# Fewer picked sets, more gathered chunks, and gathers placed behind evictions in a graph kernel

## The chip, the core and the metric

The kernel runs on one core of a Trainium2 chip. The engines that matter here are TensorE (PE in the profile; its weight loads are shown apart as PEld), VectorE (DVE), ScalarE (ACT), GpSimd (POOL) and SyncE (SP). Each works through its own list of instructions in order and waits on semaphores for the others. Time is device microseconds of one execution; the number given for a kernel is the median of its runs.

## The reference

One layer of message passing on a graph of 12,500 nodes with 128 features and 400,000 edges, followed by a residual sum and a layer norm. The edges come sorted by their destination `dst`; sources and types are random.

```python
Xs = X[src]
m_data = Xs @ W_data.T + b_data
m_ctrl = Xs @ W_control.T + b_control
msg = jnp.where((edge_types == 0)[:, None], m_data, m_ctrl)
agg = jax.ops.segment_sum(msg, dst, num_segments=X.shape[0])
out = agg + (X @ W_self.T + b_self)
x = _layernorm(x + jax.nn.relu(out), axis=-1)
```

## The kernel before

The sum over edges and the weights commute, so the kernel first adds up rows of `x` for every destination node and edge type, and applies the weights once per node. `x` is split into three bf16 parts that add up to the float32 value: `x3` on chip, `rows3` in DRAM (768 bytes a node).

**Chunks, windows, groups.** The edges are cut into 3125 chunks of 128, and these into NG = 25 groups of 125. A group consists of NE = 5 stretches of 5 + 20 chunks: a small window of PB = 5 chunks ("p") and a large one of EC = 20 chunks ("e"). The rows of x come to a chunk in one of two ways.

*Gathered* chunks: POOL issues one indirect DMA for each chunk (`fetch`, line 721), which brings the 128 source rows of its edges from `rows3` to a tile `msg`. PE adds them up by destination with three matmuls (line 677) against a 0/1 matrix `psel` made by DVE, and counts them with a fourth (line 753).

*Picked* sets: a whole e window of 20 chunks is handled as a set. DVE and PE rank its 2560 edges by the block of 128 nodes that their source lies in (the lines from 529 to 656) and put them into 25 slots (NQ) of 128 places; PE then picks rows of `x3` by matmuls with 0/1 matrices into PSUM tiles `got` (line 782), two slots to a pair, and ACT copies each pair to an SBUF tile `emsg` (line 793, the *eviction*; 12 in a set). PE adds them by destination (line 677) and counts (line 804). The few edges that fit no slot are gathered by one further indirect DMA of a set into the tile `last` (`spare_rows`, line 758), which is a part of the last slot.

In odd groups the fifth e window is no set: there the last p window has PL = 25 chunks, all gathered. So there are 13 x 5 + 12 x 4 = 113 sets and 13 x 25 + 12 x 45 = 865 gathered chunks.

**Buffers.** `got` has two PSUM buffers, each of one pair; `emsg` five; `msg` has HOLD = 18 tiles. `acc`, the sums of a group, has two buffers.

**Order.** The program is written out as one stream, and each engine gets its part of it in that order. The outer loop (line 991) runs over the sets w. A set has six turns (`unit`, line 813): in each, two pairs of slots are picked and evicted, and the four slots of the turn before are counted and added; the rest of a set is ended in the first turn of the next. Into this stream `merged` puts, by a fraction of the set: the gathered chunks, spread evenly over all sets from the third on (LAG = 2, line 983), the ranking for sets w+2 and w+3, the preparation of the next group's indices (`prep_p`, `prep_e`), and what a finished group still needs: `pass_on` and `finish`, which apply the weights and the norm and store four tiles of 125 nodes.

A chunk (`chunk`, line 741) lists at its place the gather of the chunk that comes AHEAD = 14 later; 14 gathers are listed ahead of the loop (line 974). Since `msg` has 18 tiles, such a gather writes to the tile of the chunk four places back, and waits until PE has read it. The spare gather of a set is listed in the set's third turn (line 825). POOL has hardly any work besides the gathers.

A chunk may only be gathered when its group's indices `codes["p", g]` are there, and a group is passed on to the next (`pass_on`, line 701) when all of its windows have been accumulated: 5 p windows and its sets.

Of the kernel before, what the change touches and what calls it, by code (L numbers as in the profile page):

```python
# [9 lines left out]
BF = mybir.dt.bfloat16  # L10
# [7 lines left out]
P = 128  # L18
D = 128
# [4 lines left out]
NG = NC // GC  # L24
GN = P * GC * N // E
PB = 5
PL = 25
EC = 20
CQ = EC // 4
NE = 5  # L30
NWIN = 2 * NE
# [12 lines left out]
NCELL = 4 * NQ  # L44
OVF = 64
TOP = 7
SB = 1
HOLD = 18
AHEAD = 14
ACC_ROWS = 99 * P  # L50
# [97 lines left out]
def evenly(units, a=0.0, b=1.0):  # L148
    return [(a + (b - a) * (k + 0.5) / len(units), u) for k, u in enumerate(units)]


def short_path(ctx, tc, const, ident, eps, wT, brow, bad, x, src, dst, etype, ws, bs, out):
    nc = tc.nc
# [11 lines left out]
    def windows(g):  # L165

        c = g * GC
        for i in range(NE):
            yield "p", i, c, PB
            yield "e", i, c + PB, EC  # L170
            c += PB + EC

    def of_p(g, i):

        return PL if g % 2 and i == NE - 1 else PB

    def edges(a, c, n):
        return a[c * P:(c + n) * P].rearrange("(p c) -> p c", c=n)

    rows_p = (NE - 1) * PB + PL  # L180
    each_e = [(g, i) for g in range(NG) for i in range(NE - g % 2)]
    raw = {}
    starts = {k: [c for kind, _, c, _ in windows(0) if kind == k] for k in "pe"}
    gap = PB + EC
# [37 lines left out]
    for kind, i, c, _ in windows(0):  # L222
        if kind == "p":
            n = PL if i == NE - 1 else PB
            nc.sync.dma_start(
                out=near_i[i * PB:i * PB + n, :],
                in_=dst.rearrange("(o g e) -> o g e", o=1, g=NG)[:, :, c * P].to_broadcast([n, NG]),
# [6 lines left out]
    rows3 = dram.tile([N, 3 * D], BF, name="rows3")  # L234
# [181 lines left out]
    codes = {}  # L416
# [61 lines left out]
    def select(sel, col, code2):  # L478

        rows, n, width = sel.shape  # L480
        shape = [rows, n, width // 2, 2]
        nc.vector.tensor_tensor(  # L482
            sel.rearrange("p n (w t) -> p n w t", t=2),
            col[:rows].rearrange("p (o w t) -> p o w t", o=1, t=2).to_broadcast(shape),
            code2.rearrange("p n (o t) -> p n o t", o=1).to_broadcast(shape),
            op=OP.is_equal,
        )
        return sel
# [178 lines left out]
    acc, added, parts_in = {}, [], {}  # L667

    def sums():
        return ps2.tile([P, 512], FP, name="sums")  # L670

    def cells_of(ps, width, k):
        return ps[:, k * 2 * width:(k + 1) * 2 * width]

    def add_rows(out, msg, sel, start, stop):
        for j in range(3):
            nc.tensor.matmul(  # L677
                out, msg[:, j * D:(j + 1) * D], sel, start=(start and j == 0), stop=stop, skip_group_check=True
            )
# [20 lines left out]

    def pass_on(g):

        assert parts_in[g] == NWIN - g % 2
        if g + 1 < NG:
            begin_acc(g + 1)
            added.append(nc.vector.tensor_add(acc[g + 1][:, :, :lap], acc[g + 1][:, :, :lap], acc[g][:, :, GN:]))
# [8 lines left out]
        added.append(nc.vector.tensor_add(win, win, ps[:, :4 * wide].rearrange("p (a w) -> p a w", w=wide)[:, :, :width]))  # L715


    to_fetch = [(g, i, c) for g in range(NG) for i in range(NE) for c in range(0, of_p(g, i), SB)]
    fetched = []

    def fetch():
        if to_fetch:
            g, i, c = to_fetch.pop(0)
            msg = mp.tile([P, SB, 3 * D], BF, name="msg")
            for k in range(min(SB, of_p(g, i) - c)):
                at = i * PB + c + k
                nc.gpsimd.indirect_dma_start(  # L727
                    out=msg[:, k, :], out_offset=None, in_=rows3[:, :],
                    in_offset=bass.IndirectOffsetOnAxis(ap=codes["p", g][0][:, at:at + 1], axis=0),
                )  # L730
            fetched.append(msg)

    def gathered(g, i):
        n = of_p(g, i)
        s = {}

        def choose():
            sel = sp.tile([P, PL, 2 * PW], BF, name="psel")[:, :n]
            s["sel"] = select(sel, near_col, codes["p", g][1][:, i * PB:i * PB + n])

        def chunk(c):
            if c % SB == 0:
                fetch()
                s["msg"] = fetched.pop(0)
            if c == 0:
                s["ps"] = sums()
                choose()
            sel = s["sel"][:, c].rearrange("p (t w) -> p t w", t=2)
            rows, cnt = (
                cells_of(s["ps"], AW, k).rearrange("p (t w) -> p t w", t=2)[:, :, DPC * c:DPC * c + PW] for k in range(2)  # L750
            )
            add_rows(rows, s["msg"][:, c % SB, :], sel, c == 0, c == n - 1)
            nc.tensor.matmul(cnt, one_col, sel, start=False, stop=(c == n - 1), skip_group_check=True)  # L753
            if c == n - 1:
                accumulate(g, 2 * i, s["ps"], AW, PW + DPC * (n - 1))

        return evenly([lambda c=c: chunk(c) for c in range(n)])

    def spare_rows(w):
        msg = slots[w]["last"] = two.tile([P, 3 * D], BF, name="last")  # L760
        nc.gpsimd.indirect_dma_start(  # L761
            out=msg[:OVF, :], out_offset=None, in_=rows3[:, :],
            in_offset=bass.IndirectOffsetOnAxis(ap=slots[w]["idx"], axis=0),
        )

    def picked(w, tiled, ending, fin_used, before):

        g, i = each_e[w]  # L770
        s = {"sel": {}, "msg": {}}
        per, pair = 4, 2

        def choose(q0, n=8):

            sel = select(sp.tile([P, 9, 2 * EW], BF, name="esel")[:, :n], code_col, slots[w]["code"][:, q0:q0 + n])
            for k in range(n):
                s["sel"][q0 + k] = sel[:, k]

        def pick(ps, q, a0=0):  # L780
            for a in range(a0, 4):
                nc.tensor.matmul(  # L782
                    ps[CAP * a:CAP * (a + 1), :], slots[w]["pick"][:, a * NQ + q, :],
                    x3[:, 4 * q + a - a0].rearrange("p j d -> p (j d)"), start=True, stop=True, skip_group_check=True,
                )

        def rows(q):
            ps = psg.tile([P, pair, 512], FP, name="got")
            msg = two.tile([P, pair, 3 * D], BF, name="emsg", bufs=5)
            for k in range(pair):  # L790
                pick(ps[:, k, :3 * D], q + k)
                s["msg"][q + k] = msg[:, k, :]
            nc.scalar.copy(msg, ps[:, :, :3 * D])  # L793

        def last_rows():
            q = NQ - 1
            ps = psg.tile([P, pair, 512], FP, name="got")[:, 0] if fin_used else ps1.tile([P, 512], FP, name="fin")
            pick(ps[:, :3 * D], q, 2)
            nc.scalar.copy(s["msg"][q][OVF:, :], ps[OVF:, :3 * D])

        def count(q):
            if q == 0:
                s["ps"] = sums()
            nc.tensor.matmul(  # L804
                cells_of(s["ps"], EW, 1)[CAP * (q % 4):CAP * (q % 4 + 1), :], one_col[:, :CAP], s["sel"][q],
                start=(q < 4), stop=(q + 4 >= NQ), skip_group_check=True,
            )

        def add(q0, q1):
            for q in range(q0, q1):  # L810
                add_rows(cells_of(s["ps"], EW, 0), s["msg"].pop(q), s["sel"][q], False, q == NQ - 1)

        def unit(t):

            for q in range(t * per, (t + 1) * per, pair):
                rows(q)
            if t == 1 and before:
                before()
            if t in (0, 1):
                choose(8 * t)  # L820
            if t == 0:
                ending()
            if t == 2:
                if w > 0:
                    spare_rows(w)
                s["msg"][NQ - 1] = slots[w]["last"]
            if t == 3:
                choose(16, 9)
            if t > 0:
                for q in range((t - 1) * per, t * per if t < turns - 1 else NQ):  # L830
                    count(q)
            if t == turns - 1:
                last_rows()
            if t > 0:
                add((t - 1) * per, t * per)
            for u in tiled.get(t, []):
                u()

        def end():

            add((turns - 1) * per, NQ)
            for u in tiled.get(turns, []):
                u()
            accumulate(g, 2 * i + 1, s["ps"], EW, EW)

        turns = (NQ - 1) // per
        return evenly([lambda t=t: unit(t) for t in range(turns)]), end


# [111 lines left out]
    mp = ctx.enter_context(tc.tile_pool(name="msg", bufs=HOLD))  # L961
# [9 lines left out]
    load(1, "p")  # L971
    for u in prep_p(0):
        u()
    for _ in range(AHEAD):
        fetch()


    chunks, closed, rest = {}, {}, []
# [1 line left out]
    n = 0  # L980
    for p in range(NG * NE):
        for _, u in gathered(*divmod(p, NE)):
            at = LAG + (n + 0.5) * (pairs - LAG) / total
            chunks.setdefault(int(at), []).append((at % 1, u))
            n += 1
        closed.setdefault(int(at), []).append(p)

    def ending():
        pass

    for w in range(pairs):
        g, i = each_e[w]
# [197 lines left out]
```

## Time and profile before

| | |
|---|---|
| time before, median of 3 runs (lowest, highest) | 2089.18 us (2087.51, 2096.8) |
| time of the profiled execution | 2084.42 us |
| its span, first to last instruction | 2082.7 us |
| mean granted clock of PE over the span | 0.986 |
| DMA traffic | 254.92 MB, mean 122 GB/s |
| sets / gathered chunks | 113 / 865 |

The page gives the busy time of each engine and its share of the span, then groups of instructions: line, engine, operation, what is written and read, the shapes and the count; behind the bar the busy time, the mean duration of one in ns, and the idle time of the engine just before them with what ended it. A wait is put down to the instruction whose semaphore came last. Matmuls are pipelined, so the busy time of PE covers more than the time in which its array is full, and the ends of matmuls are modelled. Line 677 is a helper of two callers; the tiles tell them apart: `esel,emsg` of picked sets, `psel,msg` of gathered chunks. Where lines of the profile are shown in windows, the columns are the length of the window, then busy us and instructions (x) of PE, PEld, DVE, ACT and POOL, the granted clock, the busy share of the DMA engines and GB/s.

### The profile page before, as it was taken

The numbers are of one execution on the slowest core, as the hardware profiler recorded it, in microseconds if no ns is written. First come the engines' busy times: TensorE is split into PE (matmuls) and PEld (weight loads), VectorE is DVE, ScalarE is ACT, GpSimd is POOL, SyncE is SP. The second block draws the span as 40 slices with busy tenths as digits, with TensorE's granted clock in tenths as the row PEclk, the third lists the DMA queues.
The fourth block names the chain that finished last, engine by engine and source line by source line (L and its number), as shares of the span: only waits on it lengthen the run. The fifth ranks groups of instructions, "written<-read, shape, count | busy, mean of one in ns | idle before, by whom it ended". The sixth has DMA issues, their size and how long they took to land.

```text
span 2082.7 us, 75459 instructions
## 1 busy us (share of the span) xinstructions
PE 1828.3 (88%) x30869; PEld 1369.9 (66%) x30869; DVE 1718.1 (82%) x4707; ACT 1304.3 (63%) x2464; POOL 1296.7 (62%) x996
## 2 busy tenths in 40 slices
PE   0489889999999998899998999999999999999996
PEld 0367666676666776676666666766776676776675
DVE  7689788988887888888888888878888888888873
ACT  3466666666665666666566666656666666766665
POOL 0446567667667667567666566676676676665660
PEclk9999999999999999999999999999999999999998
DMA  7534343443443443433433434434434434434331
GB/s 213 185 107 134 107 136 102 139 136 98 135 136 97 135 131 102 133 121 112 126 105 118 130 101 134 133 101 134 133 97 132 136 99 132 134 107 132 122 98 33
DMA packets 186535, 254.92 MB, mean 122 GB/s; under 512 B 85369, under 2 KB 152995, under 8 KB 183108
## 3 DMA queue, kind: packets, MB, share of 16 engines
q1 hardware_dynamic: 128418, 152.97, 22.7%
q0 software_dynamic: 45136, 90.65, 15.5%
q10 hardware_dynamic: 12626, 6.40, 1.1%
q8 instruction: 243, 3.98, 0.8%
q14 instruction: 112, 0.92, 0.1%
HBM read 231.89 MB, written 18.04 MB: 120 GB/s over the span
## 4 chain that ended last, share of the span: by engine, by line
PE 56%; DVE 30%; ACT 5%; issue 4%; DMA 2%; another core or an unknown queue 1%; DVEq 1%; SPq 0%; ACTq 0%
PE sums L677 24%; PE got L782 18%; ACT emsg L793 4%; DVE esel L482 4%; PE rk L620 3%; DVE pick L662 3%; DVE prod L570 3%; DVE rv L608 3%; PE sums L804 2%; DVE found L579 2%; DVE prod L548 2%; DVE ahead L566 2%; PE rk L556 2%; PE rk L508 1%; DVE half L575 1%
## 5 line engine op out<-in xcount | busy, mean ns | idle before, releaser
L727 POOL DMA_INDIRECT msg<-rows,pidx x865 | 1153.9, 1334 | 619.9 <-PE sums L677 251.9
L793 ACT CAST emsg<-got 128x768 bf16<-128x768 f32 x1356 | 1035.6, 802 | 494.2 <-PE got L782 371.4
L677 PE MATMUL sums<-esel,emsg 128*128 128x176 bf16 x8136 | 755.5, 241 | 11.4 <-issue 10.8
L782 PE MATMUL got<-x,pick 128*32 128x384 bf16 x10896 | 664.7, 332 | 91.8 <-ACT emsg L793 60.8
L677 PEld LDWEIGHTS <-emsg 128*128 128x128 bf16 x8136 | 598.1, 98 | 169.0 <-issue 152.5
L782 PEld LDWEIGHTS <-pick 128*32 128x32 bf16 x11074 | 260.8, 95 | 255.3 <-issue 156.0
L482 DVE TENSOR_TENSOR esel<-code_col,code 128x1408 bf16<-128x1408 bf16 x339 | 308.9, 911 | 29.0 <-PE sums L677 13.6
L715 DVE TENSOR_TENSOR acc<-acc,sums 128x352 f32 (+2 forms) x238 | 102.0, 429 | 169.2 <-PE sums L677 79.7
L761 POOL DMA_INDIRECT last<-rows,idx x113 | 138.7, 1227 | 132.8 <-DMA bias<-b_parts 71.3
L677 PE MATMUL sums<-psel,msg 128*128 128x48 bf16 x2595 | 186.0, 184 | 12.2 <-DVE acc L715 7.8
L804 PE MATMUL sums<-esel,one_col 128*32 128x176 bf16 x2825 | 183.5, 242 | 9.0 <-issue 8.4
L677 PEld LDWEIGHTS <-msg 128*128 128x128 bf16 x2595 | 149.1, 97 | 21.0 <-issue 18.1
L620 PE MATMUL rk<-rv,O 128*128 128x64 bf16 x2260 | 90.5, 195 | 68.0 <-DVE rv L608 63.8
L662 DVE TENSOR_SCALAR pick<-pick,lane_f 128x1600 bf16<-128x1600 bf16 x226 | 142.8, 637 | 6.8 <-DMA pick<-there 4.2
L482 DVE TENSOR_TENSOR O<-cell_col,blk 128x2000 bf16<-128x2000 bf16 x113 | 134.7, 1192 | 15.1 <-PE fin L782 6.3
L753 PE MATMUL sums<-psel,one_col 128*128 128x48 bf16 x865 | 145.3, 183 | 0.2 <-issue 0.2
L620 PEld LDWEIGHTS <-O 128*128 128x128 bf16 x2260 | 83.2, 100 | 93.9 <-issue 92.9
L570 DVE TENSOR_TENSOR prod<-O,ahead 128x2000 bf16<-128x2000 bf16 x113 | 134.4, 1190 | 0.0
L804 PEld LDWEIGHTS <-one_col 128*32 128x32 bf16 x2825 | 86.6, 96 | 45.8 <-issue 16.7
L566 DVE TENSOR_REDUCE ahead<-rk 128x100 bf16<-128x500 f32 x113 | 76.2, 675 | 48.6 <-PE rk L498 21.3
L753 PEld LDWEIGHTS <-one_col 128*128 128x128 bf16 x865 | 82.7, 96 | 1.2 <-issue 1.1
L579 DVE TENSOR_REDUCE found<-half 128x20 f32<-128x520 bf16 x113 | 77.4, 685 | 0.0
(173 smaller groups left out, 2026.6 us busy)
## 6 DMA issues: line engine op xcount, KB each, us to landing
pick<-there SPq DMA_DIRECT2D x113, 800.0 KB
acc<-acc_start SPq DMA_DIRECT2D x23, 1280.0 KB
msg<-rows,pidx POOLq DMA_INDIRECT x865
rows<-x SPq DMA_DIRECT2D x6, 1344.0 KB
xs<-in_x_dram SPq DMA_DIRECT2D x99, 62.5 KB
out_dram<-h SPq DMA_DIRECT2D x99, 62.5 KB
xt<-in_x_dram ACTq DMA_DIRECT2D x6, 896.0 KB
there<-cell SPq DMA_DIRECT2D x113, 6.2 KB
```

Source lines behind the costliest of these rows:

```text
L482: nc.vector.tensor_tensor(sel.rearrange("p n (w t) -> p n w t", t=2), col[:rows].rearrange("p (o w t) -> p o w t", o=1, t=2).to_broadcast( ...
L570: nc.vector.tensor_tensor(prod, s["O"], ahead.rearrange("p (o j) -> p o j", o=1).to_broadcast([P, EC, NCELL]), op=OP.mult)
L579: nc.vector.tensor_reduce(found, half[:, :, :26], AX.X, OP.add)
L620: nc.tensor.matmul(s["rk"][:m, :2 * CAP], s["held"][:, c * NCELL:c * NCELL + m], s["rv"][:, c].rearrange("p v r -> p (v r)"), start=(c == ...
L662: nc.vector.tensor_scalar(t, t, lane_f, None, op0=OP.is_equal)
L677: nc.tensor.matmul(out, msg[:, j * D:(j + 1) * D], sel, start=(start and j == 0), stop=stop, skip_group_check=True)
L727: nc.gpsimd.indirect_dma_start(out=msg[:, k, :], out_offset=None, in_=rows3[:, :], in_offset=bass.IndirectOffsetOnAxis(ap=codes["p", g][0] ...
L753: nc.tensor.matmul(cnt, one_col, sel, start=False, stop=(c == n - 1), skip_group_check=True)
L761: nc.gpsimd.indirect_dma_start(out=msg[:OVF, :], out_offset=None, in_=rows3[:, :], in_offset=bass.IndirectOffsetOnAxis(ap=slots[w]["idx"], ...
L782: nc.tensor.matmul(ps[CAP * a:CAP * (a + 1), :], slots[w]["pick"][:, a * NQ + q, :], x3[:, 4 * q + a - a0].rearrange("p j d -> p (j d)"), ...
L793: nc.scalar.copy(msg, ps[:, :, :3 * D])
L804: nc.tensor.matmul(cells_of(s["ps"], EW, 1)[CAP * (q % 4):CAP * (q % 4 + 1), :], one_col[:, :CAP], s["sel"][q], start=(q < 4), stop=(q + 4 ...
```

## The change

Three things are changed.

1. Which groups have a fifth set. A new function `sets(g)` gives five sets to every third group (9 groups) and four to the others (16). There are now 9 x 5 + 16 x 4 = 109 sets and 9 x 25 + 16 x 45 = 945 gathered chunks; four sets (80 chunks) have become gathered ones.
2. Where a gather is listed. The chunk no longer lists one. `due` holds, for each gather, the place of the chunk 14 before it. After each eviction `paced` lists at most one gather: a spare one if there is one, otherwise the next message gather if its due place has been reached. A dependency on that eviction is added by hand, so the gather waits for it on the chip.
3. The spare gather is handed over at the start of the set's second turn, so it stands behind the first eviction of that turn, and no longer in the third turn.

The constant SB (chunks in one `msg` tile), which was 1, goes; with it one loop that ran once.

```diff
-SB = 1
...
+    def sets(g):
+
+        return NE if g % 3 == 0 else NE - 1
+
     def of_p(g, i):
 
-        return PL if g % 2 and i == NE - 1 else PB
+        return PL if sets(g) < NE and i == NE - 1 else PB
...
-    each_e = [(g, i) for g in range(NG) for i in range(NE - g % 2)]
+    each_e = [(g, i) for g in range(NG) for i in range(sets(g))]
...
-        assert parts_in[g] == NWIN - g % 2
+        assert parts_in[g] == NE + sets(g)
...
-    to_fetch = [(g, i, c) for g in range(NG) for i in range(NE) for c in range(0, of_p(g, i), SB)]
-    fetched = []
+    to_fetch = [(g, i, c) for g in range(NG) for i in range(NE) for c in range(of_p(g, i))]
+    fetched, due, spare = [], [], []
 
     def fetch():
...
+        g, i, c = to_fetch.pop(0)
+        msg = mp.tile([P, 3 * D], BF, name="msg")
+        at = i * PB + c
+        fetched.append(msg)
+        return nc.gpsimd.indirect_dma_start(
+            out=msg, out_offset=None, in_=rows3[:, :],
+            in_offset=bass.IndirectOffsetOnAxis(ap=codes["p", g][0][:, at:at + 1], axis=0),
+        )
+
+    def paced(now, gate):
+
+        if spare:
+            gather = spare.pop()()
+        elif to_fetch and due[len(due) - len(to_fetch)] <= now:
+            gather = fetch()
+        else:
+            return
+        tc.add_manual_dep(
+            gather.ins, gate.ins.name,
+            mybir.DependencyInfo(mybir.DependencyClass.Sync, mybir.DependencyReason.DATA), reason="paced",
+        )
...
         def chunk(c):
-            if c % SB == 0:
-                fetch()
-                s["msg"] = fetched.pop(0)
+            s["msg"] = fetched.pop(0)
...
-            nc.scalar.copy(msg, ps[:, :, :3 * D])
+            paced(w + (q + 1) / (turns * per), nc.scalar.copy(msg, ps[:, :, :3 * D]))
...
         def unit(t):
 
+            if t == 1 and w > 0:
+                spare.append(lambda: spare_rows(w))
...
             if t == 2:
-                if w > 0:
-                    spare_rows(w)
+                assert not spare
                 s["msg"][NQ - 1] = slots[w]["last"]
...
-    for _ in range(AHEAD):
-        fetch()
...
             at = LAG + (n + 0.5) * (pairs - LAG) / total
             chunks.setdefault(int(at), []).append((at % 1, u))
+            due.append(at)
             n += 1
         closed.setdefault(int(at), []).append(p)
+
+    due[:] = [0.0] * AHEAD + due[:-AHEAD]
+    for _ in range(AHEAD):
+        fetch()
```

## The prediction

> **What bounds the kernel now.** I read the page's head first, then the waits of PE, then the windows of single sets, then two stretches of the timeline.
>
> ```profile
> span 2082.7 us, 75459 instructions
> PE 1828.3 (88%) x30869; PEld 1369.9 (66%) x30869; DVE 1718.1 (82%) x4707; ACT 1304.3 (63%) x2464; POOL 1296.7 (62%) x996
> ...
> L727 POOL DMA_INDIRECT msg<-rows,pidx x865 | 1153.9, 1334 | 619.9 <-PE sums L677 251.9 <-PE got L782 192.1 <-issue 84.7
> L793 ACT CAST emsg<-got 128x768 bf16<-128x768 f32 x1356 | 1035.6, 802 | 494.2 <-PE got L782 371.4 <-PE sums L677 54.9 <-remote 27.7
> ```
>
> PE is nearest to its limit, DVE close behind; POOL is idle for a third of the time, waiting for PE. The waits of PE (columns: total us, times, longest us) name what it loses:
>
> ```profile
> PE rk L620 <- DVE rv L608: 63.8, 44, 19.0
> PE got L782 <- ACT emsg L793: 60.8, 105, 7.7
> ```
>
> The second is a loop of two PSUM buffers: a pair of picked products is copied out by ACT (802 ns, line 793) before PE may write that buffer again. Startup and the end put aside, PE works some 15 of 17 us in a set. Next the windows, one set each, from its first eviction to that of the next set (columns: us, busy time of PE, PEld, DVE, ACT, POOL, in brackets the instructions):
>
> ```profile
> 106.90:122.50 15.60, 14.70 (x228) 10.44 (x227) 14.50 (x41) 11.26 (x24) 2.61 (x2) 0.85 0.28 99
> 139.40:156.40 17.00, 14.37 (x251) 10.41 (x247) 12.48 (x34) 10.51 (x20) 11.79 (x11) 1.00 0.32 103
> 1204.00:1221.10 17.10, 15.69 (x273) 11.72 (x274) 12.90 (x31) 10.41 (x19) 12.23 (x10) 1.00 0.38 107
> ```
>
> The first is the second set, still ahead of the gathered chunks: one chunk on PE and two gathers on POOL. The other two have eight chunks and ten gathers each and last 1.4 to 1.5 us longer. Sets that also carry the finishing of a group last about 20.5 us; their number, 24, and what they do stay.
>
> **Part 1: four sets fewer, 80 chunks more.** Removed: 4 sets, each with 12 evictions, 72 plus 3 adding matmuls, 98 picks, 25 counts, the ranking on DVE, one spare gather and two DMAs on SP. Added: 80 chunks, each one gather of 1334 ns and four matmuls.
> - Price of a chunk in time: from the windows, (17.05 - 15.60) / 7 more chunks = 0.21 us, which includes what eight more gathers disturb. Price of a set without chunks: 15.60 - 0.21 = 15.4 us. So -4 x 15.4 + 80 x 0.21 = -61.6 + 16.8 = **-45 us**.
> - Upper price of a chunk: its rows in the groups, 186.0 / 865 for the three message matmuls and 145.3 / 865 for the counting one, 0.38 us. A set without its chunks is then 17.05 - 7.65 x 0.38 = 14.1 us, and the sum -56.4 + 30.4 = -26 us.
> - Lower price: two chunks that follow each other on PE start 0.11 us apart (1005.19 and 1005.30 below), since four matmuls of 48 columns overlap. A set is then 16.2 us and the sum -64.8 + 8.8 = -56 us.
>
> ```profile
> 1005.19 0.25 PE L677 MATMUL sums<-psel,msg 128*128 128x48 bf16 x3
> 1005.27 0.18 PE L753 MATMUL sums<-psel,one_col 128*128 128x48 bf16 x1
> 1005.30 0.23 PE L677 MATMUL sums<-psel,msg 128*128 128x48 bf16 x3
> 1005.38 0.18 PE L753 MATMUL sums<-psel,one_col 128*128 128x48 bf16 x1
> ```
>
> I take the windows, which measure time and not busy time. DVE does not stand in the way: a set costs it some 13 us, and each of four more wide windows only (780 - 278) ns for psel and (645 - 315) ns for its accumulation, 3.3 us in all against about 50 removed.
> POOL gains 80 x 1.334 = 107 us and loses 4 x 1.23. It is hidden behind PE only as long as POOL keeps up. A set will hold (931 + 107) / 107 = 9.7 gathers; with the 0.30 us that lies before each even when nothing is waited for, that is 9.7 x 1.64 = 15.9 us of POOL in a set of about 17.5 on average, and 16.7 where no group is finished. The lead of 14 chunks (14 x 17.6 / 8.8 = 28 us) takes up the unevenness.
>
> **Part 2: gathers behind evictions.** No instruction is added. Before, a gather stands in POOL's queue where chunk c is listed and waits until PE has read the buffer of chunk c-4, so it can run up to 18 chunks ahead. After, it stands behind an eviction and waits for that ACT instruction; the wait on PE is covered by it, so in the built program the adding and message matmuls that signal a semaphore fall from 1145 to 294. Behind a waiting gather stand on POOL only other gathers and spare rows. Who waits for those is PE: the chunk 14 places later (18 evictions, 1.5 sets, some 26 us) and the last five slots of the set. The spare gather moves one sixth of a set forward, past two or three message gathers, and now waits just behind DVE's idx; its reader is over 10 us away. SP's queue and ACT's keep their order. That is a cost of nothing, hidden by 26 us; were the cover gone, each chunk would wait for a gather and its landing, about 3 us.
> What can change is the phase of gathers against PE's signals, and the trace shows that this matters:
>
> ```profile
> 730.43 0.83 PE L782 MATMUL got<-x,pick 128*32 128x384 bf16 x16
> ...
> 730.70 0.95 POOL L727 DMA_INDIRECT msg<-rows,pidx  x1 [0.30 <-issue]
> ...
> 731.95 2.66 POOL L727 DMA_INDIRECT msg<-rows,pidx  x1 [0.30 <-issue]
> ...
> 733.00 0.80 ACT L793 CAST emsg<-got 128x768 bf16<-128x768 f32 x1 [2.52 <-PE sums L677]
> ```
>
> The first pair of products was done by about 730.94, yet ACT, idle, starts on it at 733.00; usually it starts 0.1 us after the pair. In the semaphore records PE's signals reach the waiting engine 14 ns after the modelled end when no gather is near. Of those that fall between 0.2 and 1.2 us after the start of a short gather (0.95 us), seven to nine in ten arrive over 0.3 us late, mostly 1.6 us after its start, 0.65 us after its end. So each gather seems to hold back PE's signals for over a microsecond. After the change a gather starts about 0.4 us after an eviction ends, when both signals of that pair are out; the next pair's come 1.5 us after the eviction, inside the hold. PE needs the buffer again about 2 us after such a signal, ACT takes 0.8 of these, so a hold of up to 1.2 us costs nothing. I see no sign in it and take **0**. Bounds: all 60.8 us that PE waits for evictions may go, or as much may come.
>
> By the Trainium skill (TensorE: Matmul & The Clock Gate, The cost: per-tile semaphore tail) semaphore increments of matmuls serialize, at about 26 ns each. In this trace the message matmul that carries one is followed by the next after 25 ns, like the two before it that carry none, so I see no such cost; by that rule 851 increments fewer would be an estimated 22 us more gained.
>
> **The sum.** The profiled execution took 2084.4 us (span 2082.7 and 1.7 around it); -45 + 0 gives 2039.4. The median shown, 2089.2, is 4.8 above that execution, so 2044.
>
> **Rivals.**
> 1. The new phase frees PE: the waits for evictions vanish and the 61 us go besides: 2044 - 61 = 1983, or about 2000 for most of it. For it: gathers no longer start at random against the pairs. Against: 12% more of them in a set.
> 2. Slower: every gather behind an eviction holds the next pair's signal, at one place, line 793's start. It decides when the hold passes the 1.2 us of slack; from there each 0.1 us costs 109 x 6 turns x 0.1 = 65 us, so 2044 + 65 = 2109. For it: signals inside the hold by construction, two gathers in a row that can join their holds. Against: most holds are 0.4 to 1.2 us.
> 3. The gain is eaten by POOL. Its demand decides from the point where a gather takes 1.57 us instead of 1.33 (DVE's wide instructions already stretch many beyond 0.95): 9.7 x (1.57 + 0.30) = 18.1 us a set, and the 106 sets that have gathers, with the 107 us before them and the 50 us behind, last 2076, so 2082 with the 1.7 and the 4.8. For it: a demand of 15.9 us already where a set takes 16.7. Against: POOL's average stays under PE's, and the lead is long. About 2075 to 2095.
>
> By the Trainium skill (SBUF — State Buffer, SBUF: two separate sides, the box on the "DVE blocks DMA" trap) GpSimd cannot write descriptors while VectorE holds the port that they share; that would be rival 3's lengthening. The trace agrees as far as it goes: 0.95 us for most gathers between 87 and 104 us, 1.33 on average.
>
> **How the numbers follow.** Forecast, part 1 between its bounds and a quarter of part 2's 61 us either way, 2018 to 2065: 0.55. Rival 1: 0.20. Rival 2: 0.13. Rival 3: 0.12. Half a per cent, 10 us, is about what this measurement tells from no change. Faster by more: 0.55 + 0.20 + a quarter of rival 3 = 0.78; within: 0.09; slower: 0.13. The range runs from 2000, halfway into rival 1, to 2092, which leaves out rival 2.
>
> **What would show it.** Right: sets with no finishing stay within 0.4 us of 16.7; POOL busy rises by about 100 us; PE's wait for line 793's copy (805 then) stays near 60; PE busy falls by some 30. Rival 1: that wait falls below 30. Rival 2: ACT's idle time before evictions grows and sets lengthen everywhere. Rival 3: message matmuls wait for msg's DMA and POOL shows hardly a gap. A different count of PE's stalls on DVE (rk, acc) would mean that I looked at the wrong engine.

## The result, and the profile after

The changed kernel takes 2290.05 us (median of 4 runs, 2279.72 to 2290.38), the kernel before 2092.99 us beside it (4 runs). The ratio is 1.0929 with an interval of 1.0883 to 1.0976: slower by 197 us, where 45 us less were forecast.

One thing is needed to read all that follows. The experiments ran in five jobs, each with the kernel before beside them. In the runs on record and in the first two jobs the kernel before had medians of 2089 to 2104 us; in the last three the same program had 1939 to 1951 us, and the last of these ran on the same chip as the first job, that of e1 to e4. I call the first condition *holding* and the second *free*, for what the traces show in them. Each ratio below compares runs of one job, so of one condition.

First the head of the page of the changed kernel, the row of granted clock in 40 slices, and the rows that answer to those shown of before:

```profile
span 2277.5 us, 74112 instructions
...
PE 1910.9 (84%) x30253; PEld 1397.4 (61%) x30253; DVE 1681.2 (74%) x4583; ACT 1262.1 (55%) x2392; POOL 1347.0 (59%) x1072
...
PEclk9889999999899999999999999999999998999999
...
L729 POOL DMA_INDIRECT msg<-rows,pidx x945 | 1204.8, 1275 | 685.1 <-ACT emsg L805 408.7
L805 ACT CAST emsg<-got 128x768 bf16<-128x768 f32 x1308 | 996.8, 804 | 645.5 <-PE got L794 364.3
...
L794 PE MATMUL got<-x,pick 128*32 128x384 bf16 x10512 | 692.3, 342 | 154.0 <-ACT emsg L805 90.9
```

PE has 616 matmuls fewer and is busy 83 us longer. Every engine has a smaller share of the span than before; nothing has become a new bound. POOL, which rival 3 would have full, is idle for longer than before (685 us in front of gathers, against 620). ACT's idle time before evictions has grown by 151 us. And PE's clock, 0.986 before, is 0.946.

Next the four largest waits of PE (total us, times, longest us):

```profile
PE got L794 <- ACT emsg L805: 90.9, 179, 6.3
PE got L794 <- issue: 57.3, 160, 1.1
PE sums L680 <- issue: 55.3, 141, 4.3
PE rk L623 <- DVE rv L611: 36.9, 13, 19.1
```

The first was 60.8. The second and third are pauses in which PE waits for nothing that the profile shows; over all lines of PE these come to 141 us, before to 52. In the same view of before the two stand lower, and the prediction passed over them:

```profile
PE got L782 <- issue: 24.9, 78, 1.0
PE sums L677 <- issue: 15.2, 49, 0.8
```

Then three sets of the changed kernel in windows (columns as before; the first two finish no group, the third does):

```profile
878.90:898.60 19.70, 16.39 (x273) 11.80 (x271) 13.56 (x35) 11.00 (x22) 14.20 (x10) 0.98 0.36 111
1137.10:1160.00 22.90, 18.86 (x282) 12.79 (x277) 14.43 (x38) 10.93 (x22) 14.93 (x13) 0.93 0.32 94
1326.00:1351.20 25.20, 23.88 (x330) 19.04 (x329) 17.79 (x53) 14.62 (x32) 11.25 (x9) 0.83 0.35 112
```

The first does the work of the set at 1204.0 before (273 matmuls each) at nearly full clock, and lasts 2.6 us longer, of which 0.7 is PE's busy time and the rest is PE at rest. The third is nearly all busy, but at a clock of 0.83: its matmuls are slower. Between startup and end the mean set went from 16.7 to 19.3 us without a finishing, and from 20.4 to 22.7 with one.

Last, one late pair in the timeline of the changed kernel (start, duration, engine, line, what; in brackets the idle time before):

```profile
674.62 1.17 PE L794 MATMUL got<-x,pick 128*32 128x384 bf16 x16
...
674.85 0.95 POOL L729 DMA_INDIRECT msg<-rows,pidx  x1 [0.31 <-issue]
...
676.11 1.35 POOL L729 DMA_INDIRECT msg<-rows,pidx  x1 [0.30 <-issue]
676.22 0.54 PE L680 MATMUL sums<-esel,emsg 128*128 128x176 bf16 x5 [0.17 <-issue]
...
676.97 0.39 PE L680 MATMUL sums<-esel,emsg 128*128 128x176 bf16 x3 [0.21 <-issue]
...
677.72 0.31 PE L680 MATMUL sums<-esel,emsg 128*128 128x176 bf16 x2 [0.36 <-issue]
677.76 0.95 POOL L729 DMA_INDIRECT msg<-rows,pidx  x1 [0.30 <-issue]
...
679.29 1.50 ACT L805 CAST emsg<-got 128x768 bf16<-128x768 f32 x2 [4.82 <-PE sums L680]
...
680.14 0.83 PE L794 MATMUL got<-x,pick 128*32 128x384 bf16 x8
```

The row of 16 matmuls is two pairs; the second is done at 675.8, the first earlier. Three gathers follow each other with 0.3 us between them, and ACT, idle for 4.82 us, starts the two evictions 3.5 us after the second pair, 0.58 us after the third gather ends. PE picks again only when that eviction has freed the buffer. The profile puts ACT's wait down to an adding matmul, but not because the `emsg` buffer was still being read: the adds that read it stand ahead of this pair in PE's order. In between, PE's adding matmuls go on, but in small lots with pauses. Such a pause of PE falls into 0.42 of the 228 late evictions of this trace (as defined below) and 0.32 of the 179 before, from the end of the pair to the start of its eviction; in the others PE goes on and only its signal is late, as in the lines shown of before.

### The profile page after: what moved, and what is told of

It is laid out like the page before. It is cut to its first block, busy times and chain, and to the rows that moved or that the text cites. A ratio compares the mean times of both kernels' runs of the same rounds, so it can differ in the third digit from the quotient of the medians.

```text
span 2277.5 us, 74112 instructions
## 1 busy us (share of the span) xinstructions
PE 1910.9 (84%) x30253; PEld 1397.4 (61%) x30253; DVE 1681.2 (74%) x4583; ACT 1262.1 (55%) x2392; POOL 1347.0 (59%) x1072
## 4 chain that ended last, share of the span: by engine, by line
PE 59%; DVE 15%; issue 9%; ACT 8%; another core or an unknown queue 4%; DMA 2%; POOL 2%; DVEq 0%; SPq 0%; POOLq 0%; ACTq 0%
PE sums L680 24%; PE got L794 22%; ACT emsg L805 6%; PE rk L623 3%; PE sums L816 2%; PE fin L915 2%; DVE esel L485 2%; DVE prod L573 2%; POOL msg L729 1%; PE rk L559 1%; DVE pick L665 1%; PE rk L511 1%; PE rk L501 1%; DVE rv L611 1%
## 5 line engine op out<-in xcount | busy, mean ns | idle before, releaser
L729 POOL DMA_INDIRECT msg<-rows,pidx x945 | 1204.8, 1275 | 685.1 <-ACT emsg L805 408.7
L805 ACT CAST emsg<-got 128x768 bf16<-128x768 f32 x1308 | 996.8, 804 | 645.5 <-PE got L794 364.3
L794 PE MATMUL got<-x,pick 128*32 128x384 bf16 x10512 | 692.3, 342 | 154.0 <-ACT emsg L805 90.9
L680 PE MATMUL sums<-esel,emsg 128*128 128x176 bf16 x7848 | 774.7, 247 | 42.6 <-issue 40.2
L485 DVE TENSOR_TENSOR esel<-code_col,code 128x1408 bf16<-128x1408 bf16 x327 | 298.7, 914 | 58.5 <-PE sums L680 26.1
L680 PE MATMUL sums<-psel,msg 128*128 128x48 bf16 x2835 | 200.6, 186 | 25.7 <-issue 13.1
L680 PEld LDWEIGHTS <-msg 128*128 128x128 bf16 x2835 | 161.7, 99 | 42.8 <-issue 40.2
L765 PE MATMUL sums<-psel,one_col 128*128 128x48 bf16 x945 | 156.5, 185 | 4.2 <-issue 4.2
L765 PEld LDWEIGHTS <-one_col 128*128 128x128 bf16 x945 | 91.9, 97 | 4.0 <-issue 4.0
L631 ACT CAST cell<-rk 128x64 bf16<-128x64 f32 x109 | 23.3, 214 | 117.8 <-PE got L794 37.9
```

The costliest lines, as they stand in the source:

```text
L485: nc.vector.tensor_tensor(sel.rearrange("p n (w t) -> p n w t", t=2), col[:rows].rearrange("p (o w t) -> p o w t", o=1, t=2).to_broadcast( ...
L680: nc.tensor.matmul(out, msg[:, j * D:(j + 1) * D], sel, start=(start and j == 0), stop=stop, skip_group_check=True)
L729: return nc.gpsimd.indirect_dma_start(out=msg, out_offset=None, in_=rows3[:, :], in_offset=bass.IndirectOffsetOnAxis(ap=codes["p", g][0][: ...
L794: nc.tensor.matmul(ps[CAP * a:CAP * (a + 1), :], slots[w]["pick"][:, a * NQ + q, :], x3[:, 4 * q + a - a0].rearrange("p j d -> p (j d)"), ...
L805: paced(w + (q + 1) / (turns * per), nc.scalar.copy(msg, ps[:, :, :3 * D]))
```

## The experiments

Four readings were taken from each trace, the first between 130 us after the start and 30 us before the end, the others over the whole span:

- *slow clock*: time in which the granted clock is half;
- *late*: evictions that start over 0.6 us after both their pair was done and ACT was free: how many, and how many us late together;
- *emsg*: PE's wait for evictions;
- *pauses*: PE's waits on "issue", all lines.

| kernel (holding) | median us | ratio in its job | slow clock us | late, us | emsg us | pauses us |
|---|---|---|---|---|---|---|
| before (on record) | 2089 | 1 | 24 | 179, 204 | 60.8 | 52 |
| changed (on record) | 2290 | 1.0929 [1.0883, 1.0976] | 215 | 228, 349 | 90.9 | 141 |
| sets alone (e1) | 2180 | 1.0432 [1.0392, 1.0472] | 119 | 210, 285 | 42.8 | 132 |
| place and wait alone (e2) | 2181 | 1.0433 [1.038, 1.0485] | 75 | 230, 307 | 82.4 | 93 |
| changed, no wait (e3) | 2179 | 1.0452 [1.0383, 1.0522] | 119 | 209, 286 | 49.5 | 128 |
| changed, no gathers (e4) | 1878, one run | | 0 | 2, 9 | 11.0 | 4 |
| before, no gathers (e5) | 1925, one run | | 3 | 3, 3 | 9.5 | 3 |
| before, 80 more gathers (e6) | 2231 | 1.0614 [1.0544, 1.0685] | 140 | 219, 290 | 63.0 | 130 |
| changed, wait for the pick (e7) | 2215 | 1.055 [1.0493, 1.0608] | 143 | 194, 245 | 62.7 | 109 |
| 113 sets, wait for the pick (e8) | 2129 | 1.0141 [1.0095, 1.0187] | 48 | 171, 210 | 59.9 | 80 |

The kernel before had 2090.81 us in the job of e1 to e4 and 2104.32 in that of e5 to e8. The expectations name the theories that stood then: that the place behind an eviction puts the next pair's signals into the time in which a gather holds them (H; from e4 on, more widely, that the gathers and their number cost); that the number of gathers in a set costs (G); that the new list costs (L); that fewer sets are worth little or their new order costs (S); and, in e7 and e8, that what costs is gathers that follow each other at once, so that their holds join (C), or one gather per eviction whoever releases it (P).

**One part at a time (e1, e2, e3).** e1 is the kernel before with the new `sets`, its gathers still listed by the chunks. e2 is the changed kernel with the old 113 sets. e3 is the changed kernel with gathers listed after evictions and the dependency left out.

```diff
e1, in before
+    def sets(g):
+
+        return NE if g % 3 == 0 else NE - 1
...
e2, in the changed kernel
-        return NE if g % 3 == 0 else NE - 1
+        return NE - g % 2
e3, in the changed kernel
-        tc.add_manual_dep(
-            gather.ins, gate.ins.name,
-            mybir.DependencyInfo(mybir.DependencyClass.Sync, mybir.DependencyReason.DATA), reason="paced",
-        )
```

> Part 1 alone: 109 sets and 945 gathered chunks, gathers listed at their chunks and waiting for PE's read of the msg tile, as before. Theory H (a gather holds back PE's signals, and starting it behind an eviction puts the next pair's signal into that hold; late evictions leave PE idle and its clock is halved): about 2050 us, 2 per cent under before, granted clock near 0.98. Rival G (it is the number of gathers in a set, 9.7 against 8.7, that PE's signals and POOL don't bear): 2200 us or more, granted clock near 0.95.

> Part 2 and 3 alone: 113 sets and 865 chunks, each gather listed behind an eviction and waiting for it. Theory H: slower than before by about as much as the whole change or more, 2250 to 2330 us, granted clock near 0.95. Rival G: within 1 per cent of before, about 2095 us.

> The changed kernel without the dependency on the eviction: the gathers stand at the same places of POOL's list and wait only for PE's read of their msg tile, as before the change. Theory H: the wait decides, so about 2050 us. Rival L (the list itself does it: at most one gather behind each eviction, the spare gather earlier): about 2280 us as the changed kernel.

None of the three times came out as either theory had it. Both parts cost, 89 and 90 us, and together they make most of the 197. e3 equals e1 within their intervals: the new place in the stream costs nothing by itself, and neither does the spare gather's move; the wait is what costs in part 2. The waits of PE in e1 show where part 1 lost:

```profile
PE rk L624 <- DVE rv L612: 59.8, 40, 19.1
PE got L786 <- issue: 58.0, 147, 2.1
PE got L786 <- ACT emsg L797: 42.8, 76, 4.7
PE sums L681 <- issue: 35.9, 87, 1.2
```

The wait for evictions is 18 us smaller than before; it is PE's pauses that grew, from 52 to 132 us over all lines, and the slow clock, from 24 to 119 us. In e2 both rows grew, pauses by 40 and emsg by 22.

**No message gathers at all (e4, e5).** After the first 14 gathers, `fetch` gives the chunks those 14 tiles again and lists none. The sums of the gathered chunks are then of the wrong rows; every other instruction stays.

```diff
+        if len(first) == AHEAD:
+            fetched.append(first[len(to_fetch) % AHEAD])
+            return None
...
+        first.append(msg)
```

> The changed kernel without its message gathers, but for the first 14: the chunks read these 14 tiles again and again, so 931 gathers are left out and the sums of gathered chunks are those of other rows. The spare gathers stay. Theory H: PE's signals come in time, PE's wait for evictions falls from 91 us to under 30, the granted clock is about 0.99 and the time 1900 to 1980 us. If something else in the new order slows PE (not the gathers), the time stays above 2150 us.

> The kernel before without its message gathers, but for the first 14: chunks read these 14 tiles again and again, 851 gathers are left out, the spare ones stay. Beside the changed kernel without gathers (1878 us) it prices four sets against 80 chunks when nothing holds PE's signals. Theory H (the gathers take back what part 1 gains): 1878 + 45 to 56 = 1923 to 1934 us. Rival S (fewer sets are worth little by themselves, or the new distribution of groups costs something): 1870 to 1900 us.

e4's rows of evictions and picks:

```profile
L811 ACT CAST emsg<-got 128x768 bf16<-128x768 f32 x1308 | 990.2, 803 | 355.7 <-PE got L800 339.5
...
L800 PE MATMUL got<-x,pick 128*32 128x384 bf16 x10512 | 595.6, 330 | 15.1 <-ACT emsg L811 11.0
```

Without gathers there are hardly any late signals, pauses or slow clock, and ACT's idle time before evictions is 356 us where it was 646. Between the two kernels without gathers lie 47 us (one run of each, in different jobs) in favour of the changed one: four sets with their work against 80 chunks with theirs, the trade that the prediction had put at 45. But the gathers themselves are dear: 851 of them cost the kernel before 2104 - 1925 = 179 us, about 0.21 each, and the 931 of the changed kernel cost 2290 - 1878 = 412. What leaves with them is the work on POOL and the moving of the bytes alike; these two runs do not tell them apart.

**80 more gathers in the kernel before (e6).** Into a tile that nobody reads, spread over the program; `msg` has 17 tiles to make room.

```diff
-HOLD = 18
+HOLD = 17
...
+            n = 865 - len(to_fetch)
+            if n > AHEAD and n * 80 // 851 > (n - 1) * 80 // 851:
+                more = mp.tile([P, 3 * D], BF, name="more", bufs=1)
+                nc.gpsimd.indirect_dma_start(
+                    out=more, out_offset=None, in_=rows3[:, :],
...
```

> The kernel before with 80 more gathers, spread evenly, into one tile that nobody reads (msg has 17 tiles and not 18, to make room). No set and no chunk is changed. Theory H (the number of gathers is what part 1 costs): 2090 + 90 + 45 = about 2200 to 2240 us, granted clock about 0.965. Rival S: about 2100 us, and the cost of part 1 lies in the sets' new order.

No set is taken away and PE has not one instruction more, and it costs 127 us: 1.6 us a gather, over seven times the mean of the 851 that are there. What was averaged at 0.21 is steep at the margin. With it part 1 comes out: -47 for the work and +127 for 80 gathers give +80, and e1 measured +89. Two things besides the number changed in e6: `msg` has a tile less, and POOL waits 61 us in all for the one tile of the added gathers to be free. PE waits for a gathered `msg` tile 0.2 us in all there, so neither reaches it as late data; a kernel with the smaller `msg` alone was not run.

**Another event to wait for (e7, e8).** The gather waits for the last pick of the pair on PE, and no longer for the copy on ACT. e8 is e7 with 113 sets.

```diff
-                pick(ps[:, k, :3 * D], q + k)
+                picked_last = pick(ps[:, k, :3 * D], q + k)
...
-            paced(w + (q + 1) / (turns * per), nc.scalar.copy(msg, ps[:, :, :3 * D]))
+            nc.scalar.copy(msg, ps[:, :, :3 * D])
+            paced(w + (q + 1) / (turns * per), picked_last)
```

> The changed kernel, where the gather listed behind an eviction waits for the last pick of that pair (PE) and no longer for the eviction (ACT). Theory C (ACT's signals are not held, so gathers released by ACT run one behind the other while PE's signals are still held, which lengthens the hold; a gather that waits for a PE signal can only start when held signals have come out): 2150 to 2190 us, as without the wait or a little less. Rival P (one gather a turn at this place of the stream, whoever releases it): 2270 to 2300 us.

> The same wait for the last pick with the 113 sets and 865 chunks of before. Theory C: 2060 to 2100 us, no slower than before, perhaps a little faster, since a gather then starts right behind a pair's signals. Rival P: about 2180 us, as with the wait for the eviction.

The event decides: with 113 sets +25 us instead of +90, and on the changed kernel 2215 instead of 2290. So neither one gather per eviction nor a wait as such costs the 90, but this release; whether by the moment at which it comes or by the engine that gives it, these runs do not tell apart. The modelled ends of pairs speak for the moment: of the pair signals, the share that falls between 0.7 us before the end of a gather and 0.3 us behind it is 0.40 in the kernel before, 0.51 in e2, 0.50 in the changed kernel, 0.39 in e8 and 0.42 in e7. Gathers strewn at random would give some 0.45 to 0.49 in each (an estimate: their number times 1 us, over the span). So the wait for the eviction puts the share above chance, and the wait for the pick below it, where the old wait of the kernel before has it too. It is no measure of the whole loss: e1, e3 and e6, where no gather waits for an eviction, have 0.47 to 0.48, near chance, and lose about 90 us (e1, e3) and 127 (e6), and e7 loses 111 at 0.42. Both numbers of the expectation were missed (2215 against 2150 to 2190, 2129 against 2060 to 2100), and so was theory C: gathers that follow one another at once are 0.55 of all before, 0.64 in e2, 0.63 in e8 and 0.69 in e7, so e8 bunches as much as e2 and costs little over a quarter of it.

**117 sets, thinner gathers, a longer lead (e9, e10, e11; then f3, f4, g1, g2).** e9 goes the other way, two thirds of the groups with five sets (785 gathers). e10 is the changed kernel with gathers of 256 bytes a row in place of 768, so that its message sums are of thirds of other rows, each taken three times. e11 is the kernel before with a lead of 17 chunks.

```diff
e9, in e1
-        return NE if g % 3 == 0 else NE - 1
+        return NE - 1 if g % 3 == 1 else NE
e10, in the changed kernel
-            out=msg, out_offset=None, in_=rows3[:, :],
+            out=msg[:, :D], out_offset=None, in_=rows3.rearrange("n (j d) -> (n j) d", d=D),
...
e11, in before
-AHEAD = 14
+AHEAD = 17
```

> The other way: groups with five sets but every third with four, so 117 sets and 785 chunks, gathers placed and waiting as in the kernel before. Priced by the runs: without gathers four sets more cost 47 us; 80 gathers more cost 127 to 137 us beside before, while all 851 cost 166. Theory H (each further gather costs more, since PE's stalls also halve its clock): 80 fewer save 40 to 70 us, so 2070 to 2095 us, with no stretch at half clock in the loop. If a gather costs the same everywhere at the margin (1.6 us): 2010 us. If the holds hardly matter below 865 gathers: about 2135 us.

> The changed kernel with gathers of 256 bytes a row and not 768: as many gathers with as many rows each, a third of the bytes. Rows are then other ones than the edges', and the three message matmuls all read that third. If the writing of the descriptors and their start holds PE's signals: 2230 to 2300 us, as the changed kernel. If the moving of the bytes does: 1878 + 412 / 3 = about 2015 us.

> The kernel before with gathers listed 17 chunks ahead and not 14; msg keeps 18 tiles, so a gather waits until PE has read the chunk just before and no longer the fourth before. If what matters is that a gather starts right on a fresh signal of PE (as with the wait for the pick): within 1.5 per cent of before, either way. If bunches of gathers that run one behind the other are the harm: 2040 to 2070 us, since each then follows a chunk of its own.

This job met the free condition: the kernel before took 1939.15 us (17 runs). So none of these tests of the hold could decide: there was none. e9 took 1985.29, ratio 1.0242 [1.021, 1.0274]; e11 1945.81, ratio 1.0027 [1.0009, 1.0045]; e10 1923.69 in one run. Each trace has at most one late eviction.

**The same kernels in the free condition (f1 to f4, g1 to g3).** f1 is the changed kernel unaltered, f2 is e2, f3 and g1 are e9, f4 and g2 are e10, g3 is e1.

> The changed kernel once more, beside before on whatever chip it meets. On a chip that holds PE's signals behind gathers (before near 2090 us): 2270 to 2300 us. On one that doesn't (before near 1939 us): theory H says that then only part 1's price of sets and chunks is left, 1939 - 47 = 1892 us; if the change has another cost of its own (the order of the list, a later gather), 1920 us or more.

> 113 sets, each gather behind an eviction and waiting for it. On a chip that holds the signals: about 90 us over before. On one that doesn't: within 0.5 per cent of before.

> 117 sets and 785 chunks, gathers as before. On a chip that holds the signals: 2070 to 2095 us, no slower than before. On one that doesn't: about 46 us over before, as measured there.

> The changed kernel with gathers of a third of the bytes (the chunks' sums are then those of other rows). On a chip that holds the signals: 2230 to 2300 us if the writing of descriptors holds them, about 2015 us if the moving of the bytes does. On one that doesn't: within 2 per cent of the changed kernel there.

> 117 sets and 785 chunks. On a chip that holds PE's signals: 2070 to 2095 us, no slower than before there. On one that doesn't: 2.1 to 2.4 per cent over before, as measured twice.

> The changed kernel with gathers of a third of the bytes (the chunks' sums are then those of other rows). On a chip that holds the signals: 2230 to 2300 us if the descriptors hold them, about 2015 us if the moving of the bytes does. On one that doesn't: near 1920 us again.

> 109 sets and 945 chunks, gathers listed and waiting as before. On a chip that holds the signals: 4.3 per cent over before, as measured. On one that doesn't: 1.5 to 2.3 per cent under before, by the price of four sets (47 us) less what clock is lost.

| kernel (free) | median us | before beside it | ratio | late | emsg us | pauses us |
|---|---|---|---|---|---|---|
| changed (f1) | 1922.09 | 1950.78 | 0.9825 [0.9778, 0.9873] | 0 | 10.1 | 0 |
| place and wait alone (f2) | 1948.53 | 1950.78 | 0.9978 [0.996, 0.9997] | 0 | 11.9 | 0 |
| sets alone (g3) | 1925.65 | 1949.49 | 0.9884 [0.982, 0.9947] | 0 | 10.3 | 0 |
| 117 sets (f3) | 1995.89 | 1950.78 | 1.0208 [1.0169, 1.0247] | 0 | | 0 |
| 117 sets (g1) | 1991.76 | 1949.49 | 1.0212 [1.0166, 1.0258] | 0 | | 0 |
| thin gathers (f4; g2) | 1919.99; 1925.65, one run each | 1950.78; 1949.49 | | 1; 1 | | |

The job of g1 to g3 ran on the chip of e1 to e4, and still in the free condition. In that condition the changed kernel is faster by 29 us, 1.75%, and part 1 alone by 24. Both are less than expected: theory H had 1892 for f1, and a cost of the change's own from 1920 up, and 1.5 to 2.3% under the kernel before for g3, which has 1.16. As f2 takes what the kernel before takes, what is missing of the 47 us lies in part 1 and not in the place and the wait. f2, f3, f4, g1 and g2 came as expected for a free chip. The head of f1, its gathers and its picks:

```profile
span 1934.4 us, 74112 instructions
...
PE 1725.0 (89%) x30253; PEld 1329.5 (69%) x30253; DVE 1668.4 (86%) x4583; ACT 1262.3 (65%) x2392; POOL 1448.4 (75%) x1072
...
L729 POOL DMA_INDIRECT msg<-rows,pidx x945 | 1288.1, 1363 | 328.0 <-issue 151.8
...
L794 PE MATMUL got<-x,pick 128*32 128x384 bf16 x10512 | 601.7, 333 | 12.2 <-ACT emsg L805 10.1
```

The same 74112 instructions take 343 us less. POOL is busier (gathers are, if anything, longer: 1363 ns against 1275), PE 186 us less busy and hardly ever waiting for an eviction. Four pairs beside gathers in its timeline:

```profile
942.25 0.83 PE L794 MATMUL got<-x,pick 128*32 128x384 bf16 x16
...
942.87 1.50 ACT L805 CAST emsg<-got 128x768 bf16<-128x768 f32 x2 [0.50 <-PE got L794]
...
943.02 1.53 POOL L729 DMA_INDIRECT msg<-rows,pidx  x1 [0.30 <-DVE idx L522]
...
944.66 0.83 PE L794 MATMUL got<-x,pick 128*32 128x384 bf16 x16
...
944.86 5.03 POOL L773 DMA_INDIRECT last<-rows,idx  x1 [0.30 <-issue]
...
945.28 1.50 ACT L805 CAST emsg<-got 128x768 bf16<-128x768 f32 x2 [0.91 <-PE got L794]
```

The last two pairs are done within a gather of 5.03 us, the spare one, and their evictions start 0.62 us after the first of their matmuls, as for the two pairs before them. In the trace of f1 a larger share of pair signals falls into the end of a gather (0.55) than in any kernel of the holding condition, and not one eviction is late.

The thin gathers take what the changed kernel takes, in the free condition. 117 sets cost 42 to 46 us more than 113 (e9, f3, g1) and 109 cost 24 us less; so in both directions four sets are worth some tens of us once the gathers hold nothing.

## Why the prediction was wrong

**What bounds the kernel.** That the loop of the two `got` buffers is where PE loses was right, but only one of its two rows was read. PE's pauses (52 us before) belong to the same cause: in e4 and e5, without gathers, and in the free condition, they all but vanish (0 to 4 us) together with the late evictions, and the waits for evictions fall to 9 to 12 us.

**Part 1, the step that failed first.** "Price of a chunk in time: from the windows, (17.05 - 15.60) / 7 more chunks = 0.21 us, which includes what eight more gathers disturb." As the price of 80 more chunks it was wrong: e6 shows 1.6 us for the gather alone, and the upper price, 0.38, does not reach it either. The windows stood at two and at ten gathers a set, and nothing in them told what further gathers cost where sets hold nearly nine on average. That the mean of the 851 gathers is 0.21 as well (179 us) does not bear the price out, for the 0.21 of the prediction was to cover a chunk's matmuls too. It was low for a second reason: the window of 15.60 us ran at a clock of 0.85, the other two at 1.00. At full clock it would last some 2.3 us less (an estimate: 30% of it at half rate, half of that lost), a chunk would be 0.54 us and a set 12.7, and the sum about -8 us. So it is in part luck that the -45 lies so near the 47 us between e5 and e4, which are four sets against 80 chunks with no gathers at all. The measured part is +89 instead of -45.

**Part 2, the second.** "PE needs the buffer again about 2 us after such a signal, ACT takes 0.8 of these, so a hold of up to 1.2 us costs nothing. I see no sign in it and take 0." The place was read rightly: signals of the next pair inside the hold by construction, which was rival 2 with a chance of 0.13. What failed is the allowance. In the trace of the changed kernel the last signal of PE ahead of an eviction comes over 1.20 us behind the end of its pair in a quarter of the cases (before: over 0.68; in e4, without gathers: 0.03), and one eviction in ten starts over 1.12 us late (before: 0.69), so a signal often uses up the 1.2 us, as in the timeline above. The bounds, 60.8 us either way, were drawn from emsg alone; e2 measured +90, of which the pauses (+40) are the larger share beside emsg (+22).

**Rival 2's price.** It gave 2109 and the direction; the size lacked the pauses, the trade of part 1 and the clock.

**The clock, which no step had.** The time at half rate went from 24 to 215 us. Matmuls at half rate lose half of that time if PE has work through it, so this is an estimated (215 - 24) / 2 = 96 us. PE's idle time grew from 156 to 277 us in the stretch read, 121 us. Four sets against 80 chunks take 44 us of PE's busy time off (1745.4 in e5, 1701.4 in e4), so this makes 121 + 96 - 44 = 173 of the 195 us between the two spans. The same sum gives 69 + 48 - 44 = 73 of 91 for e1 (idle 225), 57 + 26 = 83 of 100 for e2 (idle 213) and 86 + 58 = 144 of 140 for e6 (idle 242). So about half of the loss came as waits and pauses of PE, and most of the rest as matmuls at half rate; some 20 us of the 195 are not accounted for. By the Trainium skill (TensorE: Matmul & The Clock Gate, Part 1: The HAM clock gate) the default rate is half, and PE's activity in windows of some 3.4 us decides; the stretches here are multiples of 3.4 us long. In the 3.4 us ahead of each of the 44 stretches of the changed kernel PE was busy for 0.55 of the time (median; between startup and end 0.93), and in three quarters of the cases its longest single rest there was under 1.1 us. So many small rests go before them, seldom a long one. That PE's pauses at the gathers are what brings these rests is how I read it: kernels with more pauses have more of these stretches, from 0 in e4 to 215 us in the changed one, though f1, with no pauses, still has 55.

**What was right.** Rival 3 fell: POOL is idle longer, and message matmuls hardly wait for their DMA. That fewer semaphore signals of the adding and message matmuls gain nothing was right too: f2, which has 847 fewer of PE's, is 2 us under the kernel before. And where signals are not held, the forecast holds in sign and partly in size: -29 us for the changed kernel against -45, part 1 alone -24, part 2 alone -2.

**What stays open.** What sets the condition was not found; it is not the chip, since one chip showed both. Whether the hold goes with the bytes or with the number of a gather's rows could not be told, since the thin gathers ran in the free condition alone; nor was the version with 117 sets seen in the other. That a gather itself holds PE's signals rests on the two kernels without gathers and on where late signals lie against gather ends; how it does so no trace shows, nor whether PE's pauses are the same hold or a second effect. No version beat both kernels in both conditions: of those that do the whole work the kernel before is the best in the one; in the other the changed kernel and part 1 alone lead, and their intervals overlap.

## What to carry to other kernels

A mean price taken from what is there is not the price of one more: where a cost comes from two streams that disturb each other, double or add the one in a kernel of its own before trading work for it. When a wait is added, ask not only who stands behind it but what happens on the other engines at the moment of its release; a different event for the same wait changed its cost from 90 to 25 us. And add up PE's waits for nothing ("issue") with the named ones, and look at its granted clock, since small gaps return as slow matmuls.

## What was not expected of the hardware

- Late signals were PE's alone, as far as they are recorded. The recorded signals of DVE and ACT come 8 to 13 ns after the end of an instruction that gives one in 99 of 100 cases, beside gathers too; about a fifth of theirs left no record.
- The same program on the same chip took 2091 us in one job and 1949 in another. Its trace on record, of the first condition, has 179 late evictions; of the second no trace of it was kept, and those of the other kernels there have at most one each. Without gathers, in the first condition and on another chip, it took 1925.
- Half-rate stretches add up to 215 us in a kernel whose PE is 84% busy; its 160 pauses before picks are at most 1.1 us long, its 179 waits for evictions 0.5 us on average.
